# First attention's node table and turned edge lists moved ahead of the branch on the edge list's order

## Chip, cores and metric

The kernel runs on one core of a Trainium2 chip. The metric is device microseconds of one execution. The four runs of the kernel before have a median of 7833.06 us (7821.41 to 7836.81).

## What is computed

The input is a graph of 6250 nodes with 256 features each and a list of 206,250 edges (`src`, `dst`, sorted by `dst`). Four layers follow one another, and each adds its result to `x`. The change touches only the first one, a graph attention with 4 heads of 64 columns:

```
h = (layernorm(x) @ W).reshape(N, H, C)
a_src = einsum('nhc,hc->nh', h, att_src);  a_dst = einsum('nhc,hc->nh', h, att_dst)
e = leaky_relu(a_src[src] + a_dst[dst])
p = exp(e - segment_max(e, dst)[dst])
out = segment_sum(p / segment_sum(p, dst)[dst] * h[src], dst)
x = x + relu(out + bias)
```

After it come a mixture of 8 experts (top 2), a weighted sum over the same edges, and a second attention with a mixture of 4 experts.

## The kernel before, in words

The 6250 nodes are 49 tiles of 128 rows. `X` holds all of them in SBUF for the whole kernel; eight DMAs on the ACT queue load it (L2190, L2191). The kernel has two ways to compute the result: `fast` (from L1835), which relies on the edges being almost evenly spread over the sorted `dst`, and `general`, which doesn't. What decides is a look at the list.

**The look** is `check_stream` (L1032 to L1109). It copies `dst` into a padded DRAM list, reads it back shifted by one place and by other offsets (L1055, L1056, L1059, L1081, one after the other into two buffers), and compares on VectorE in tiles of 128x1664. On the way it writes the list as float (`dl_d`, L1069), as 16-bit integers (L1067), a mark of equal neighbours (L1060) and a mark of each node's last edge (`last_d`, L1072) to DRAM. Its last instruction writes `flag` (L1109). Each engine reads the flag into a register (L2197) and takes the branch.

**Behind the branch** `fast` first makes what the attention's stream needs. *The turned lists* (L1852 to L1868): `src` is loaded, negative or too large numbers are mended on VectorE, and `turn_rows` (L1111) transposes 13 blocks of 128x128 on TensorE, with ScalarE copying from PSUM; the same for `dl_d` (less the first node of each window, L1157 to L1176) and for `last_d`. The results `si`, `dl`, `il` stay in SBUF. *The table* (L1870 to L1896): `W` and the two attention vectors are loaded on the ACT queue, eight columns that give `a_src` and `a_dst` are made from them, and then the nodes go through in 7 chunks of 7 tiles: layernorm on VectorE (L247 to L257), two transposes per tile on TensorE and a copy on ScalarE (`transposed`, L259), two matmuls (L1890, four records a tile in the profile), a copy to `tb` on ScalarE (L1891), a copy of four columns to `NI` on VectorE (L1892), one store of each chunk to the DRAM tensor `tab` on the SP queue (L1893) and two small VectorE operations on `NI` (L1895, L1896).

**The stream** is `gat_stream` (L1191). It first splits `NI` into three bf16 parts (L1215 to L1219), writes them to DRAM (`s_nb`, L1221), and then runs in an order written out by hand: GpSimd gathers rows of `tab` by `si` (L1260, 1612 gathers), and the other engines work on pieces of 8 x 128 edges.

Outside that hand-written order, an automatic scheduler sets the order of each engine's instructions when the program is built: an instruction earlier in the program goes first, a later one fills in where the earlier is expected to wait. The order is then fixed, each engine runs its own in order, and nothing of a branch's body mixes with what stands outside it. DMAs issued on SP stand in SP's order, those issued on ACT in ScalarE's, between its copies. Buffers of pools that are open at different times share space, and the later one waits until the earlier is no longer in use.

Of the kernel before, what the change touches and what calls it, by code (L numbers as in the profile page):

```python
# [20 lines left out]
F32 = mybir.dt.float32  # L21
BF = mybir.dt.bfloat16
I32 = mybir.dt.int32
I16 = mybir.dt.int16
AF = mybir.ActivationFunctionType
OP = mybir.AluOpType
AX = mybir.AxisListType
PSUM = bass.MemoryType.PSUM
# [4 lines left out]
P = 128  # L33
LN_EPS = 1e-5
BIG = float(2**100)
CH = 7
# [11 lines left out]
def chunks(n, size):  # L48
    return [(i, min(size, n - i)) for i in range(0, n, size)]


def rows(ap):

    return bass.AP(tensor=ap.tensor, offset=ap.offset, ap=[[0, P], [1, ap.size()]])
# [17 lines left out]
def tile_kernel(ctx, tc, src_ins, out):  # L72
    nc = tc.nc
    x_in = src_ins["x"]
# [172 lines left out]
    def layernorm(pool, dst, src, n):  # L247

        mv = pool.tile([P, n, 2], F32, name="mv")
        for t in range(n):  # L250
            bs = pool.tile([P, 6], F32, name="bs")
            nc.vector.bn_stats(bs, src[:, t, :])
            nc.vector.bn_aggr(mv[:, t, :], bs)
        rs = rstd_of(pool, mv[:, :, 1], n)
        for t in range(n):
            nc.vector.tensor_scalar(dst[:, t, :], src[:, t, :], mv[:, t, 0:1], rs[:, t:t + 1],
                                    op0=OP.subtract, op1=OP.mult)  # L257

    def transposed(pp, dst, src, **bufs):  # L259

        pt = pp.tile([P, KD, P], F32, name="pt", **bufs)
        for k in range(KD):
            nc.tensor.transpose(pt[:, k], src[:, k * P:(k + 1) * P], ident)
        nc.scalar.copy(dst, pt)
# [405 lines left out]
    def x_rows(ap):  # L670

        for t0, n in chunks(FULL, CH):
            yield ap[t0 * P:(t0 + n) * P].rearrange("(t p) d -> p t d", p=P), X[:, t0:t0 + n, :]
        if REST:
            yield ap[FULL * P:], X[:REST, FULL, :]
# [435 lines left out]
    def turn_rows(dst, src, C):  # L1111

        with tc.tile_pool(name="turn_ps", bufs=2, space=PSUM) as pp:
            for c0, n in chunks(C, 4):
                pt = pp.tile([P, 4, P], F32, name="pt")
                for c in range(n):
                    nc.tensor.transpose(pt[:, c], src[:, c0 + c, :], ident)
                nc.scalar.copy(dst[:, c0 * P:(c0 + n) * P], pt[:, :n].rearrange("p c e -> p (c e)"))

    def load_rows(p, ap, E, C, dtype, name):  # L1120

        t = p.tile([P, C, P], dtype, name=name)
        nc.vector.memset(t[:, C - 1:, :], 0)
        a = C - 1
        nc.sync.dma_start(t[:, :a, :], ap[:a * P * P].rearrange("(c p e) -> p c e", p=P, e=P))
        left = E - a * P * P
        r = left // P
        if r:
            nc.sync.dma_start(t[:r, a, :], ap[a * P * P:a * P * P + r * P].rearrange("(p e) -> p e", p=r))
        if left > r * P:  # L1130
            nc.sync.dma_start(t[r:r + 1, a, :left - r * P], ap[a * P * P + r * P:E][None, :])
        return t
# [23 lines left out]

    def from_first_window(s, dl, p):  # L1157

        base = p.tile([P, s.C * P], F32, name="base")
        if s.group is None:  # L1160
            b0, start = s.windows(0, Q)[0][0], 0
            for q in range(-(-s.T // Q) + 1):
                b = s.windows(q * Q, min(Q, s.T - q * Q))[0][0] if q * Q < s.T else None
                if b != b0:
                    nc.gpsimd.memset(base[:, start:s.C * P if b is None else q * Q], float(P * b0))
                    b0, start = b, q * Q
        else:
            nc.gpsimd.memset(base[:, s.T:], 0.0)
            for i, n, first, step in s.runs:
                full = min(n, s.T // s.group - i)  # L1170
                if full > 0:
                    nc.gpsimd.iota(base[:, i * s.group:(i + full) * s.group], pattern=[[step, full], [0, s.group]],
                                   base=first, channel_multiplier=0, allow_small_or_imprecise_dtypes=True)
                if full < n:
                    nc.gpsimd.memset(base[:, (i + full) * s.group:s.T], float(s.wins[-1][0]))
        nc.vector.tensor_sub(dl, dl, base)  # L1176
# [655 lines left out]

    moves = {}

    def fast(flag_s0, last_d, dl_d):  # L1835
        s0 = flag_s0
        C = s0.C
        keep = ExitStack()
# [1 line left out]
        wide = moves["wide"] = kp.tile([P, 3 * P], F32, name="wide")  # L1840
        nc.vector.memset(wide, 0.0)
        nc.vector.tensor_copy(wide[:, P:2 * P], ident)
        tab = dram.tile([NP, D + H0], F32, name="tab")
        chosen_by = ExitStack()
        f0 = chosen_by.enter_context(tc.tile_pool(name="f0f", bufs=1))
        head = Head(f0)
        with tc.tile_pool(name="gat0f", bufs=1) as g0:
# [1 line left out]
            dl = g0.tile([P, C * P], F32, name="dl")  # L1849
            il = g0.tile([P, C * P], BF, name="il")  # L1850
            NI = g0.tile([P, NT, 2 * H0], F32, name="NI")
            with tc.tile_pool(name="rows", bufs=1) as p:  # L1852
                sr = load_rows(p, I["src"], s0.edges, C, I32, "sr")
                sf = p.tile([P, C, P], F32, name="sf")
                t = p.tile([P, C, P], F32, name="tt")
                nc.vector.tensor_copy(sf, sr)
                nc.vector.tensor_scalar(t, sf, 0.0, float(N), op0=OP.is_lt, op1=OP.mult)
                nc.vector.tensor_add(sf, sf, t)
                nc.vector.tensor_scalar(sf, sf, 0.0, float(N - 1), op0=OP.max, op1=OP.min)
                turn_rows(si, sf, C)  # L1860
                dr = p.tile([P, C, P], F32, name="dr")
                nc.sync.dma_start(dr, dl_d)
                turn_rows(dl, dr, C)
                from_first_window(s0, dl, p)
                lr = p.tile([P, C, P], F32, name="lr")
                nc.sync.dma_start(lr, last_d)
                turn_rows(il, lr, C)

            with tc.tile_pool(name="l0", bufs=2) as lp, tc.tile_pool(name="l0_ps", bufs=2, space=PSUM) as pp:
                wx = lp.tile([P, KD, D + 2 * H0], F32, name="wx", bufs=1)  # L1870
                nc.scalar.dma_start(wx[:, :, :D], I["L0_gnn_W"].rearrange("(k p) f -> p k f", p=P))
                att = lp.tile([P, 2, D], F32, name="att", bufs=1)
                nc.scalar.dma_start(att[:, 0], rows(I["L0_gnn_att_src"]))
                nc.scalar.dma_start(att[:, 1], rows(I["L0_gnn_att_dst"]))
                for k in range(KD):
                    for s in range(2):
                        pr = lp.tile([P, D], F32, name="pr")
                        nc.vector.tensor_mul(pr, wx[:, k, :D], att[:, s])
                        nc.vector.tensor_reduce(wx[:, k, D + s * H0:D + (s + 1) * H0],
                                                pr.rearrange("p (h c) -> p h c", h=H0), AX.X, OP.add)  # L1880
                for t0, n in chunks(NT, CH):
                    xl = lp.tile([P, CH, D], F32, name="xl")
                    layernorm(lp, xl, X[:, t0:t0 + n, :], n)
                    tb = lp.tile([P, CH, D + H0], F32, name="tb")
                    for j in range(n):
                        xT = lp.tile([P, KD, P], F32, name="xT")
                        transposed(pp, xT, xl[:, j, :])
                        ph = pp.tile([P, D + 2 * H0], F32, name="ph")
                        for k in range(KD):
                            nc.tensor.matmul(ph, xT[:, k], wx[:, k], start=(k == 0), stop=(k == KD - 1))  # L1890
                        nc.scalar.copy(tb[:, j, :], ph[:, :D + H0])  # L1891
                        nc.vector.tensor_copy(NI[:, t0 + j, :H0], ph[:, D + H0:])  # L1892
                    nc.sync.dma_start(tab[t0 * P:(t0 + n) * P].rearrange("(t p) d -> p t d", p=P), tb[:, :n])  # L1893
                    own = NI[:, t0:t0 + n, H0:]
                    nc.vector.tensor_add(own, tb[:, :n, D:], NI[:, t0:t0 + n, :H0])  # L1895
                    nc.vector.scalar_tensor_tensor(own, own, 0.2, own, op0=OP.mult, op1=OP.max)  # L1896
            bias = g0.tile([P, D], F32, name="bias")
            nc.sync.dma_start(bias, rows(I["L0_gnn_bias"]))

# [287 lines left out]

    if REST:
        nc.vector.memset(X[:, FULL, :], 0.0)
    for a, b in x_rows(x_in):  # L2190
        nc.scalar.dma_start(b, a)  # L2191
    s0 = Stream("s0", I["src"].shape[0], SLACK0, N, GROUP0, True)
    last_d = dram.tile([P, s0.C, P], F32, name="last_d")
    dl_d = dram.tile([P, s0.C, P], F32, name="dl_d")
    flag = main.tile([P, 1], I32, name="flag")
    check_stream(s0, I["dst"], flag, last_d, dl_d)
    v = nc.values_load(flag[0:1, 0:1], min_val=0, max_val=1, skip_runtime_bounds_check_because="a comparison: 0 or 1")  # L2197
    with tc.If(v == 1) as cmp:
        fast(s0, last_d, dl_d)
    with cmp.Else():  # L2200
        general()

# [22 lines left out]
```

## Time and profile before

| what | us |
|---|---|
| median of four runs | 7833.06 |
| the profiled execution, by its own time | 7850.32 |
| its span in the trace | 7848.5 |
| flag written | 66.35 to 66.51 |
| first instruction behind the branch (SP) | 67.44 |
| last turned list copied | 92.08 |
| first and last tile of the table (first transpose, last `NI` operation) | 98.80 to 170.10 |
| store of `s_nb` issued | 176.76 |
| first gather | 188.55 |

The times inside the execution count from the span's start. The profile lists busy time by engine, and for a group of instructions the time that its engine stood idle just before them and what ended this wait. PE is TensorE (PEld its weight loads), DVE is VectorE, ACT is ScalarE, POOL is GpSimd, SP issues DMAs; a `q` after the name means the engine's own queue of instructions, where DMA issues are. `PEclk` is the granted clock of TensorE as a share of full speed.

### The profile page before, as it was taken

What the parts mean: (1) busy time and instruction counts of PE and PEld (TensorE: products, weight loads), DVE (VectorE), ACT (ScalarE), POOL (GpSimd) and SP (SyncE); (2) the same over time, 40 slices, a digit from 0 to 9 for tenths busy, and PEclk for the clock granted to TensorE, in tenths of its full rate; (3) what the DMA queues carried; (4) which work ended last, traced back from release to release, by engine and by line L of the source; (5) the groups of instructions that cost most, each with busy time, mean ns of one, the idle gap of its engine ahead of it and who ended that gap; (6) DMA issues with size and microseconds to landing.
All of it is one profiled execution on the core that took longest, in us unless ns stands there. A gap on an engine that the chain in (4) does not pass through costs nothing.

```text
span 7848.5 us, 62325 instructions
## 1 busy us (share of the span) xinstructions
PE 3837.8 (49%) x17463; PEld 2905.0 (37%) x17463; DVE 4465.4 (57%) x10655; ACT 1160.3 (15%) x2758; POOL 4103.3 (52%) x4320
## 2 busy tenths in 40 slices
PE   3355555555555699994235555555555641111111
PEld 2244434343433488873123333343433421111110
DVE  4355555555555753434576666666766615665666
ACT  2011111111111123221001222221211210000000
POOL 0666666666666232320666666666666355555552
PEclk9677777776777799997567777777777865555555
DMA  4444444444444165575333333333333212222221
GB/s 126 117 120 121 119 116 113 113 119 115 121 116 118 55 204 187 185 227 179 98 93 100 96 100 100 101 101 96 99 99 97 72 41 46 50 47 46 46 49 41
DMA packets 496233, 821.82 MB, mean 105 GB/s; under 512 B 143345, under 2 KB 315588, under 8 KB 495843
## 3 DMA queue, kind: packets, MB, share of 16 engines
q0 software_dynamic: 190880, 462.26, 22.6%
q1 hardware_dynamic: 292326, 343.79, 14.3%
q10 hardware_dynamic: 12668, 11.68, 0.5%
q8 instruction: 141, 2.31, 0.1%
q14 instruction: 218, 1.78, 0.1%
HBM read 743.27 MB, written 77.29 MB: 105 GB/s over the span
## 4 chain that ended last, share of the span: by engine, by line
DVE 20%; PE 18%; another core or an unknown queue 13%; issue 9%; ACT 2%; DMA 2%; POOL 1%; ACTq 0%; DVEq 0%; SPq 0%; POOLq 0%
DVE run L2028 8%; PE ph L630 5%; PE py L643 5%; PE pf L1714 3%; PE pf L1725 3%; DVE X L1813 2%; DVE oh L1152 2%; PE acc L2142 1%; DVE run L2026 1%; DVE s L1345 1%; DVE g L1347 1%; DVE ot L1270 1%; DVE oh L2032 1%; ACT h L1719 0%
## 5 line engine op out<-in xcount | busy, mean ns | idle before, releaser
L234 POOL DMA_INDIRECT g<-tab_ef,si x1616 | 1540.7, 953 | 1028.0 <-issue 563.2
L1260 POOL DMA_INDIRECT g<-tab,si x1612 | 1542.5, 957 | 907.4 <-issue 544.6
L2028 DVE SCALAR_TENSOR_TENSOR run<-g,wab,run 128x256 f32<-128x256 f32 x2626 | 1264.8, 488 | 540.1 <-DVE run L2028 185.8
L1260 POOL DMA_INDIRECT g<-tab_1f,si1s x787 | 761.6, 968 | 716.6 <-issue 626.5
L1363 PE MATMUL acc<-g,oh 128*128 128x264 f32 x3224 | 989.4, 467 | 190.8 <-DVE g L1340 103.8
L1363 PEld LDWEIGHTS acc<-g,oh 128*128 128x128 f32 x3224 | 751.0, 239 | 382.5 <-DVE g L1340 117.4
L1290 DVE TENSOR_REDUCE nd<-pd 128x64 f32<-128x192 f32 (+1 forms) x301 | 106.0, 352 | 1212.6 <-remote 959.5
L1714 PE MATMUL pf<-xt,w 128*128 128x512 f32 (+1 forms) x832 | 486.7, 724 | 464.8 <-ACT h L1719 193.2
L2142 PE MATMUL acc<-run,oh 128*128 128x256 f32 x808 | 295.2, 500 | 681.0 <-DVE oh L2032 315.7
L1725 PE MATMUL pf<-w,h 128*128 128x256 f32 x1568 | 413.1, 414 | 223.1 <-ACT y L1730 93.6
L2142 PEld LDWEIGHTS acc<-run,oh 128*128 128x128 f32 x808 | 191.7, 250 | 784.1 <-issue 409.7
L1340 DVE TENSOR_TENSOR g<-g,mix 128x2048 f32<-128x2048 f32 x202 | 457.6, 2265 | 0.0
L1714 PEld LDWEIGHTS pf<-xt,w 128*128 128x128 f32 x832 | 183.4, 241 | 661.3 <-issue 310.8
L1363 PE MATMUL acc<-s,oh 128*128 128x72 bf16 x1267 | 97.0, 251 | 672.0 <-DVE s L1345 510.8
L1725 PEld LDWEIGHTS pf<-w,h 128*128 128x128 f32 x1568 | 316.1, 207 | 292.9 <-issue 104.2
L1306 PE MATMUL zt<-ident,Z 128*128 128x128 f32 x228 | 76.9, 396 | 681.3 <-ACT Z L1298 393.0
L630 PE MATMUL ph<-xe,w 128*128 128x256 f32 x1792 | 406.9, 384 | 5.1 <-DVE xe L618 5.1
L643 PE MATMUL py<-w,h 128*128 128x256 f32 x1792 | 397.3, 379 | 0.0
L630 PEld LDWEIGHTS ph<-xe,w 128*128 128x128 f32 x1792 | 342.3, 193 | 52.1 <-DVE xe L618 5.9
L643 PEld LDWEIGHTS py<-w,h 128*128 128x128 f32 x1792 | 335.7, 190 | 43.1
L1363 PEld LDWEIGHTS <-oh 128*128 128x128 bf16 x1267 | 90.4, 133 | 675.6 <-issue 581.7
L606 POOL DMA_INDIRECT xg<-tab_x,gi x112 | 126.8, 1132 | 389.1 <-PE pt L615 314.7
(506 smaller groups left out, 5931.8 us busy)
## 6 DMA issues: line engine op xcount, KB each, us to landing
w<-in_L_ffn_W SPq DMA_DIRECT2D x112, 1024.0 KB
db<-s_d SPq DMA_DIRECT2D x299, 256.0 KB
g<-tab_ef,si POOLq DMA_INDIRECT x1616
g<-tab,si POOLq DMA_INDIRECT x1612
y_d<-y SPq DMA_DIRECT2D x196, 128.0 KB
yb<-y_d SPq DMA_DIRECT2D x49, 512.0 KB
g<-tab_1f,si1s POOLq DMA_INDIRECT x787
yy<-tab_y SPq DMA_DIRECT2D x7, 1792.0 KB
```

Source lines behind the costliest of these rows:

```text
L234: nc.gpsimd.indirect_dma_start(out=dst, out_offset=None, in_=table, in_offset=bass.IndirectOffsetOnAxis(ap=si[:, t:t + 1], axis=0))
L630: nc.tensor.matmul(ph, w1[:, k, f * P:(f + 1) * P], xe[:, k, :], start=(k == 0), stop=(k == KD - 1))
L643: nc.tensor.matmul(py, hs[f][:, i * P:(i + 1) * P], w2[:, f, :], start=(f == 0), stop=(f == FC - 1))
L1152: nc.vector.tensor_tensor(o[:, :m], ips[:, None, k * P:(k + 1) * P].to_broadcast([P, m, P]), dl[:, a:a + m, None].to_broadcast([P, m, P]), ...
L1260: nc.gpsimd.indirect_dma_start(out=g[:, j, :DH + H], out_offset=None, in_=tab, in_offset=bass.IndirectOffsetOnAxis(ap=si[:, t0 + j:t0 + j ...
L1340: nc.vector.tensor_mul(gh, gh, ps[0][:, o:o + n, :, None].to_broadcast([P, n, H, CD]))
L1363: nc.tensor.matmul(acc[b].rearrange("p s w -> p (s w)"), oh[:, t - a], m_, start=(t == lo), stop=(t == hi))
L1714: nc.tensor.matmul(ph[:, :n], w1[:, e, k, f * P:(f + 1) * P], xts[g][:, k, :n], start=(k == 0), stop=(k == KD - 1))
L1725: nc.tensor.matmul(py[:, :D], hs[g, e, f][:, j * P:(j + 1) * P], w2[:, e, f, :], start=(f == 0), stop=(f == FC - 1))
L1813: nc.vector.scalar_tensor_tensor(X[:, b, :], v[:, e, :], gates[:, j, e:e + 1], X[:, b, :], op0=OP.mult, op1=OP.add)
L2028: nc.vector.scalar_tensor_tensor(at[:, i] if j < Q - 1 else r[i], g[:, j, :], w, at[:, i], op0=OP.mult, op1=OP.add)
L2142: nc.tensor.matmul(acc[i], oh[:, k], r[k], start=(q % 2 == 0 and k == 0), stop=(last and k == 1))
```

## The change

The layernorm, the table and the turned lists are taken out of `fast` and put into one block with `check_stream`, ahead of the flag's reading. They therefore run whatever the flag says. The pools of that block are open together, so that the look, the lists and the table have buffers of their own.

What was kept in SBUF now goes through DRAM: `si`, `dl`, `il` are stored (`si_d0`, `dl_d0`, `il_d0`), `NI` is stored chunk by chunk (`ni_d`), and `fast` loads the four of them. On the ACT queue `W` and the two attention vectors are loaded ahead of `X`. The copy from PSUM takes all 264 columns in place of 260, and the four columns of `NI` are then copied once a chunk in place of once a tile. Some buffers are used again: `src`'s own tile takes the turned `si`, and the tiles `tt` and `sf` take `dl_d` and `last_d`.

```diff
     def fast(...):
...
-            with tc.tile_pool(name="rows", bufs=1) as p:
-                sr = load_rows(p, I["src"], s0.edges, C, I32, "sr")
...
-            with tc.tile_pool(name="l0", bufs=2) as lp, tc.tile_pool(name="l0_ps", bufs=2, space=PSUM) as pp:
...
-                        nc.scalar.copy(tb[:, j, :], ph[:, :D + H0])
-                        nc.vector.tensor_copy(NI[:, t0 + j, :H0], ph[:, D + H0:])
...
+            for t, d in ((si, si_d0), (dl, dl_d0), (il, il_d0)):
+                nc.sync.dma_start(t, d)
+            nc.sync.dma_start(NI.rearrange("p t d -> p (t d)"), ni_d)
...
-    for a, b in x_rows(x_in):
-        nc.scalar.dma_start(b, a)
...
-    check_stream(s0, I["dst"], flag, last_d, dl_d)
+    tab = dram.tile([NP, D + H0], F32, name="tab")
+    ni_d = dram.tile([P, NT * 2 * H0], F32, name="ni_d")
+    with tc.tile_pool(name="l0", bufs=2) as lp, tc.tile_pool(name="l0_ps", bufs=2, space=PSUM) as pp:
+        wx = lp.tile([P, KD, D + 2 * H0], F32, name="wx", bufs=1)
+        nc.scalar.dma_start(wx[:, :, :D], I["L0_gnn_W"].rearrange("(k p) f -> p k f", p=P))
+        att = lp.tile([P, 2, D], F32, name="att", bufs=1)
+        nc.scalar.dma_start(att[:, 0], rows(I["L0_gnn_att_src"]))
+        nc.scalar.dma_start(att[:, 1], rows(I["L0_gnn_att_dst"]))
+        for a, b in x_rows(x_in):
+            nc.scalar.dma_start(b, a)
+        check_stream(s0, I["dst"], flag, last_d, dl_d)
...
+        si = load_rows(p, I["src"], s0.edges, C, I32, "sr")
...
+        turn_rows(si, sf, C)
+        nc.sync.dma_start(si_d0, si)
+        dl = p.tile([P, C * P], F32, name="dl", bufs=1)
+        nc.sync.dma_start(t, dl_d)
+        turn_rows(dl, t, C)
+        from_first_window(s0, dl, p)
+        nc.sync.dma_start(dl_d0, dl)
+        il = p.tile([P, C * P], BF, name="il", bufs=1)
+        nc.sync.dma_start(sf, last_d)
+        turn_rows(il, sf, C)
+        nc.sync.dma_start(il_d0, il)
...
+        for t0, n in chunks(NT, CH):
+            xl = lp.tile([P, CH, D], F32, name="xl")
+            layernorm(lp, xl, X[:, t0:t0 + n, :], n)
+            tb = lp.tile([P, CH, D + 2 * H0], F32, name="tb")
+            for j in range(n):
...
+                nc.scalar.copy(tb[:, j, :], ph)
+            nc.sync.dma_start(tab[t0 * P:(t0 + n) * P].rearrange("(t p) d -> p t d", p=P), tb[:, :n, :D + H0])
+            ni = lp.tile([P, CH, 2 * H0], F32, name="ni")
+            own = ni[:, :n, H0:]
+            nc.vector.tensor_copy(ni[:, :n, :H0], tb[:, :n, D + H0:])
...
+            nc.sync.dma_start(ni_d[:, 2 * H0 * t0:2 * H0 * (t0 + n)], ni[:, :n].rearrange("p t d -> p (t d)"))
     v = nc.values_load(flag[0:1, 0:1], ...)
     with tc.If(v == 1) as cmp:
-        fast(s0, last_d, dl_d)
+        fast(s0, si_d0, dl_d0, il_d0, tab, ni_d)
```

## The prediction

> **What bounds the kernel now.** Most of the span is gathers and what hangs on them; the change lies in the first 188.55 us, before the first gather. So I read that stretch, first by stages: the look, the lists, the table, the preparation of the stream, the stream.
>
> ```profile
> core 0: us, PE busy (x) PEld busy (x) DVE busy (x) ACT busy (x) POOL busy (x), PEclk, DMA share, GB/s
> 0.00:67.40 67.40, 0.58 (x2) 0.50 (x2) 30.34 (x29) 0.00 (x0) 2.18 (x7) 1.00 0.65 196
> 67.40:91.50 24.10, 9.62 (x39) 7.43 (x39) 8.12 (x8) 6.39 (x12) 2.33 (x6) 1.00 0.33 111
> 91.50:170.10 78.60, 62.73 (x294) 48.24 (x294) 49.58 (x226) 35.84 (x109) 0.00 (x0) 0.96 0.23 79
> 170.10:188.55 18.45, 0.00 (x0) 0.00 (x0) 3.02 (x6) 0.00 (x0) 0.59 (x6) 0.51 0.71 67
> 188.55:2400.00 2211.45, 1113.65 (x5066) 856.31 (x5066) 1140.10 (x2220) 244.69 (x683) 1399.19 (x1463) 0.72 0.44 118
> ```
>
> The stages stand one behind the other. In the first, TensorE and ScalarE do nothing and VectorE is busy for 30.3 of 67.4 us; in the third, TensorE is nearly full (62.7 of 78.6). What VectorE waits for ahead of the flag is seen in its waits:
>
> ```profile
> DVE d L1066 <- DMA lend<-s_dst: 16.9, 1, 16.9
> DVE t L1071 <- DMA lend<-s_dst: 8.4, 1, 8.4
> DVE kf L1058 <- DMA lend<-s_dst: 5.6, 1, 5.6
> DVE t L1082 <- DMA lend<-s_dst: 3.2, 1, 3.2
> ```
>
> These 34.1 us are the look's own round trips through DRAM, and they are room. What the table costs an engine stands in the groups of instructions of the first 190 us (count, busy us, mean ns, idle before):
>
> ```profile
> L1890 PE MATMUL ph<-wx,xT 128*128 128x264 f32 x196 | 51.3, 405 | 7.5 <-ACT xT L264 7.5
> L252 DVE BATCH_NORM_STATS2 bs<-X 128x6 f32<-128x256 f32 x49 | 18.5, 415 | 1.3 <-PE pt L1117 1.3
> L256 DVE TENSOR_SCALAR xl<-X,mv,rs 128x256 f32<-128x256 f32 x49 | 17.4, 410 | 1.1 <-PE pt L263 1.1
> L263 PE MATMUL pt<-ident,xl 128*128 128x128 f32 x98 | 15.4, 279 | 7.3 <-issue 7.3
> L1892 DVE COPY NI<-ph 128x4 f32<-128x4 f32 x49 | 7.8, 160 | 26.7 <-ACT tb L1891 26.1
> L253 DVE BATCH_NORM_AGGREGATE mv<-bs 128x2 f32<-128x6 f32 x49 | 6.7, 167 | 0.0
> ```
>
> TensorE's 51.3 + 15.4 us are the table's floor, and VectorE's wait of 26.1 us for ScalarE's copies says that it is not the bound there. The end of the stretch, in order of time:
>
> ```profile
> 169.91 0.19 DVE L1896 SCALAR_TENSOR_TENSOR NI<-NI 128x28 f32<-128x28 f32 x1
> ...
> 173.74 0.56 DVE L1215 CAST NB<-NI 128x392 bf16<-128x392 f32 x1 [3.43 <-DMA tab<-tb]
> ...
> 176.76 0.36 SPq L1221 DMA_DIRECT2D s_nb<-NB  x1
> ...
> 188.55 1.11 POOL L1260 DMA_INDIRECT g<-tab,si  x1 [14.11 <-DMA s_nb<-NB]
> ```
>
> From the table's end (170.10) it is 3.64 us to the split of `NI` and 18.45 to the first gather.
>
> **Rule of the sum.** From the first gather on the same instructions follow in the same hand-written order, so the change in time is the shift of the first gather. Call T the end of the table and lists after the change, and R what the split then waits. The shift is (T - 170.10) + (R - 3.64).
>
> **What is moved, by engine.** VectorE: the mending of `src` is 1.03 + 1.03 + 1.89 + 1.03, the subtraction 1.89, together 6.9 us; the eight columns 4 x (0.419 + 0.414) = 3.3; layernorm 18.5 + 6.7 + 17.4 + 1.3 for the reciprocals = 43.9, or 6.3 a chunk; the `NI` operations 3 a chunk at 0.18 (by L1895) in place of 49 copies. With the look's 30.3 that makes 88 us. The 6.5 us saved on copies are worth nothing, since VectorE was waiting there. ScalarE: 36 us of copies, and four columns more in each tile's copy (376 ns for 260) add 0.3 us in all; it waited 34.6 us for matmuls, so nothing again. TensorE: a pair of tiles takes 2.79 us (the second matmul groups start at 142.81 and 145.60), so 49 tiles 68.4 us; the turns 9.7 us (39 records in the first 24.1 us stage, 9.62). GpSimd: its five fills (2.3 us) stand in 64.7 us of idle time. SP: seven stores of the table, five loads and six stores of lists, seven of `ni_d` now stand in the same queue as the look's reads. ACT's queue: three loads ahead of `X`.
>
> **When TensorE can start.** The eight issues of `X` hold ScalarE's queue from 0.75 to 23.5 us, and each tile needs a ScalarE copy, so the table starts at about 25 us at best.
>
> **How much is done before the flag.** The look is earlier in the program, so on VectorE the layernorm has only its gaps: 34.1 us, of which the first 10 pass before `X`'s first chunk is there (an estimate: the DMAs moved 230 to 285 GB/s in that time, some 2.6 MB of mixed traffic). In the other 24 the columns (3.3) and the mending (5.0) come first, which leaves 16 us: 2.5 chunks at 6.3. The two buffers of the normalized rows allow two chunks ahead of TensorE as well. From 50 to 66 us VectorE is full, and TensorE, which needs 9.8 us a chunk, runs dry.
>
> **The flag and after.** `src`, `W` and the vectors (805 + 256 + 256 KB) come into the window in which DMA was full (285 to 385 GB/s); 1.3 MB at 330 is 4 us, so the flag comes at 70.4. Then TensorE has 9.7 us of turns (they need the look's last outputs and VectorE is at the next layernorm meanwhile) and the rest of the table: T = 70.4 + 9.7 + (49 - 7k) x 1.394 + 1.1 for the last copies, with k chunks done before. k = 2: 130.2; k = 3: 120.5; middle 125.3.
>
> Here the Trainium skill speaks against the change. The look's first reads took 9.6 us (issued at 10.04 and 10.49, landed by 20.08) beside `X`, and the last one 5.3 us (41.73 to 47.07) with nothing beside it. The page "DMA: Bandwidth & Descriptors", section "Issuing engines are not separate DMA queues", says that the DMAs of all queues run on the same 16 engines and interleave. By that rule two more reads of the look would take the longer time beside the table's stores, 2 x 4.3 us more, and the forecast below would be 9 us later.
>
> **What is added behind the branch.** SP takes the branch 1.1 us after its last issue (66.35 to 67.44 before), issues Head's two loads (0.85), then `si`, `dl`, `il` and `NI`, 2.28 MB. The nearest row are the three list loads before: 2.4 MB from 68.37 until the turn's start at 79.39, 11.0 us. Adding 0.4 for the issue of the last `ni_d` store, R = 13.4, which is 9.8 more than now. The lower end is a small load, 3.06 us (`att`, 92.71 to 95.77): R = 5.4, 1.8 more. Behind `NI`'s load SP holds `bias`, `s_nb` and the first loads of the stream; before, those stood behind `s_nb`'s landing too, so nobody else waits. I take 9.8, as the sizes are alike. The stores of the lists (2 MB) lie beside the table and cost nothing unless they lie between the look's reads.
>
> **Sum.** (125.3 - 170.1) + 9.8 = -35 us. The profiled execution's 7850.3 becomes 7815; it stands 17.3 above the median, which becomes 7833 - 35 = **7798 us**.
>
> **Rivals.**
> 1. *Everything overlaps*: VectorE serves both, and TensorE alone sets the end: 25 + 68.4 + 9.7 = 103. Shift -67.0 + 9.8 = -57, time 7776. For it: 34 us of gaps. Against: VectorE's 88 us leave little slack and the look's dense stretch comes in one piece.
> 2. *It doesn't do what it says*: the fixed order puts the layernorm behind the look (k = 0), or SP's order puts the look's reads behind stores that wait for matmuls. T = 149.5, shift -11, time 7822: no measurable difference. For it: before, the layernorm stood behind other things in every queue, and the order is set at build time from expected durations, while the reads took up to 9.6 us.
> 3. *Slower, by TensorE's clock.* Where TensorE had been idle the table began slowly: from 98 to 102 us the granted clock was 0.50, four transposes took 1.19 instead of 0.60 us and the first eight matmuls 3.05 instead of 2.05, so a pair 4.24 instead of 2.79. If the starved TensorE stayed there for the table, rival 2's 68.4 us become 104: T = 185, shift +25, time 7858. It decides from T above 176 on (shift over +15.7). For it: from 190 to 280 us, at some 5% busy, the clock was 0.50, and 0.73 to 0.76 at 50 to 60%. Against: in the table itself, 90% busy, it was 1.00, and after the flag TensorE is fed without a break.
>
> The page "TensorE: Matmul & The Clock Gate", section "What's actually happening", has it that the gate opens after about 3.4 us of sustained work and closes after an idle window of that length. In the trace the clock was back at 0.99 from 102 us on, 3.2 us after the first transpose, and had fallen to 0.54 in the stretch from 95 us on, after TensorE's last turn at 91.5. By the rule each chunk that TensorE starts after a pause costs one slow pair, 1.5 us, so two pauses 3 us, and rival 3 cannot hold.
>
> **Numbers.** Forecast (k from 1 to 4) 0.58, rival 1 0.17, rival 2 0.17, rival 3 0.08. A measurement of this kernel tells 0.2% (15.7 us) from no change. k = 1 gives T = 140 and -20.6, still faster; so faster 0.58 + 0.17 = 0.75, same 0.17, slower 0.08. The range runs from rival 1 with the small R (-65, 7768) to rival 2 with 6 us for a second slow read (7828) and leaves rival 3 out.
>
> **What would show it.** Right: transposes of layernormed rows (L263 before) from about 25 us on, a pause of TensorE until the flag, VectorE's four waits of the look filled in part, the last tile near 125, the first gather near 151. Wrong: a first transpose behind the flag (rival 2), a clock of 0.5 over tens of us (rival 3), the last tile near 103 (rival 1), or a stream that doesn't keep its 2211 us.

## The result, and the profile after

The median after is 7817.62 us (44 runs, 7788.62 to 7868.94), before 7832.67 us (68 runs, 7790.19 to 7864.72). The ratio is 0.9983, 95% interval 0.9974 to 0.9991: 13 us less, between 7 and 20, against 35 forecast. That is less than the 0.2% that the prediction called telling. The two profiled executions differ by 52 us (span 7796.3 after 7848.5). Most of this isn't the change's: the runs of one kernel spread over 75 us, and single executions say nothing at this size. The first gather tells more, because the stretch ahead of it repeats within 0.4 us (170.72 here, 170.38 in a second profile of the same kernel).

The stretch by stages, cut at the flag, the table's end, the split of `NI` and the first gather (columns as before):

```profile
core 0: us, PE busy (x) PEld busy (x) DVE busy (x) ACT busy (x) POOL busy (x), PEclk, DMA share, GB/s
0.00:74.20 74.20, 11.89 (x45) 7.74 (x45) 45.47 (x85) 6.77 (x17) 4.43 (x13) 1.00 0.71 212
74.20:140.70 66.50, 58.32 (x291) 45.54 (x290) 33.02 (x135) 34.06 (x102) 0.00 (x0) 0.97 0.38 127
140.70:154.97 14.27, 0.00 (x0) 0.00 (x0) 0.83 (x4) 0.10 (x1) 0.59 (x5) 0.60 0.70 242
154.97:170.70 15.73, 0.00 (x0) 0.00 (x0) 2.82 (x5) 0.00 (x0) 0.00 (x0) 0.50 0.73 19
170.70:2620.00 2449.30, 1241.69 (x5660) 956.64 (x5660) 1281.95 (x2511) 277.15 (x771) 1542.44 (x1612) 0.72 0.44 117
```

Ahead of the flag TensorE was busy for 11.9 us only, and six of the table's seven chunks still stand behind it (28 of its 196 matmul records lie ahead). The stream's 2449.3 us compare with 2450.5 before (from 188.5 to 2639): it kept its length in these two executions. VectorE's waits ahead of the flag show why TensorE had so little:

```profile
DVE d L1066 <- DMA lend<-s_dst: 9.5, 1, 9.5
DVE t L1071 <- DMA lend<-s_dst: 9.3, 1, 9.3
DVE pr L2190 <- DMA att<-in_L_gnn_att_src: 5.9, 1, 5.9
DVE kf L1058 <- DMA lend<-s_dst: 2.1, 1, 2.1
DVE t L1082 <- DMA lend<-s_dst: 0.6, 1, 0.6
```

27.4 us of waiting stayed, where the kernel before had 34.1; 5.9 of the 27.4 are a new wait, for `att`, ahead of the look's first read. The second of these waits, with what follows on VectorE (and ScalarE's square root), in order of time:

```profile
31.71 1.89 DVE L1058 TENSOR_TENSOR kf<-lend,lend 128x1664 bf16<-128x1664 int32 x1 [2.12 <-DMA lend<-s_dst]
...
33.60 0.49 ACT L242 ACTIVATE sd<-mv,eps 128x7 f32<-128x7 f32 x2
...
42.89 1.89 DVE L1071 TENSOR_TENSOR t<-lend,lend 128x1664 f32<-128x1664 int32 x1 [9.29 <-DMA lend<-s_dst]
...
50.29 0.19 DVE L244 RECIPROCAL rs<-sd 128x7 f32<-128x7 f32 x1
...
57.36 0.41 DVE L256 TENSOR_SCALAR xl<-X,mv,rs 128x256 f32<-128x256 f32 x1
57.82 0.69 PE L263 MATMUL pt<-ident,xl 128*128 128x128 f32 x2 [57.82 <-DVE xl L256]
58.62 0.41 DVE L256 TENSOR_SCALAR xl<-X,mv,rs 128x256 f32<-128x256 f32 x1
```

At 34.1 the square roots of two chunks are there, and VectorE stands idle for 9.3 us; but in its fixed order the reciprocal and the normalizing (L244, L256) come behind the look's L1071, and then one tile at a time between the look's steps of 1.9 us. The end of the stretch:

```profile
140.54 0.19 DVE L2209 SCALAR_TENSOR_TENSOR ni<-ni 128x28 f32<-128x28 f32 x1
140.75 0.45 SPq L2210 DMA_DIRECT2D ni_d<-ni  x1
145.23 0.38 SPq L691 DMA_DIRECT2D wr<-in_L_ffn_Wr  x1
...
147.59 0.62 SPq L1853 DMA_DIRECT2D NI<-ni_d  x1
...
154.97 0.56 DVE L1215 CAST NB<-NI 128x392 bf16<-128x392 f32 x1 [8.76 <-DMA NI<-ni_d]
...
157.96 0.38 SPq L1221 DMA_DIRECT2D s_nb<-NB  x1
...
170.72 1.11 POOL L1260 DMA_INDIRECT g<-tab,si  x1 [24.84 <-DMA s_nb<-NB]
```

So the table's end T is 140.73 (forecast 125.3), the wait R from there to the split is 14.24 (13.4), and from the split to the gather it is 15.75 (14.81 before). The shift of the first gather is 170.72 - 188.55 = -17.8 us, which lies in the interval of the timed runs.

### The profile page after: what moved, and what is told of

Its sections match the earlier page's. It is cut to its first block, busy times and chain, and to the rows that moved or that the text cites. A ratio compares the mean times of both kernels' runs of the same rounds, so it can differ in the third digit from the quotient of the medians.

```text
span 7796.3 us, 62291 instructions
## 1 busy us (share of the span) xinstructions
PE 3846.9 (49%) x17463; PEld 2906.3 (37%) x17463; DVE 4458.3 (57%) x10613; ACT 1158.6 (15%) x2757; POOL 4100.2 (53%) x4320
## 3 DMA queue, kind: packets, MB, share of 16 engines
q0 software_dynamic: 190880, 462.26, 22.6%
## 4 chain that ended last, share of the span: by engine, by line
DVE 28%; PE 26%; another core or an unknown queue 21%; issue 15%; ACT 3%; DMA 3%; POOL 2%; ACTq 1%; DVEq 0%; POOLq 0%; SPq 0%
DVE run L1985 7%; PE acc L1363 5%; PE ph L630 5%; PE py L643 5%; PE pf L1714 4%; DVE oh L1152 3%; DVE g L1340 3%; PE pf L1725 2%; POOL g L1260 2%; DVE X L1813 2%; DVE ot L1270 1%; PE acc L2099 1%; DVE run L1983 1%; PE bacc L1389 1%
```

## The experiments

Theory after the result: the change is worth the shift of the first gather and nothing else; T is late because VectorE's fixed order puts the normalizing behind the look, so that one chunk of seven was done at the flag. Rivals: ScalarE, held by the issues of `X` until 32.3 us, delays the table; VectorE has too much work in all; the stream absorbs or adds something. Times are compared with runs of the kernel before on the same chip only: the first and third group ran where that kernel takes 6481 to 6483 us, the second where it takes 7767 us.

**NI loaded first** (first group, one run).

```diff
+            nc.sync.dma_start(NI.rearrange("p t d -> p (t d)"), ni_d)
             for t, d in ((si, si_d0), (dl, dl_d0), (il, il_d0)):
                 nc.sync.dma_start(t, d)
-            nc.sync.dma_start(NI.rearrange("p t d -> p (t d)"), ni_d)
```

> The changed kernel with one edit: behind the branch the load of NI is issued ahead of the loads of si, dl and il. Theory (the split of NI waits for the 2 MB of lists in front of it on SP's queue): the table still ends near 140.7 and the branch is taken near 145.2, but the split starts near 150 in place of 154.97, and the first gather near 166 in place of 170.72, since the lists land beside the split and the store of s_nb. Rival (the four loads share the same transfer engines, so NI lands no earlier, or si becomes what the first gather waits for): split at 154 to 155, or first gather still at 170 to 171.

The split, on VectorE in order of time:

```profile
149.59 0.56 DVE L1215 CAST NB<-NI 128x392 bf16<-128x392 f32 x1 [3.22 <-DMA NI<-ni_d]
```

It starts 5.4 us earlier, the wait ahead of it is 3.2 in place of 8.8, and the first gather comes at 166.0. Of the round trip, 5 us were the place in the queue. The time was 6457.0 against 6481.3 (one run).

**Table first** (first group, five runs). The columns and the loop over the chunks are moved ahead of `check_stream`; no instruction is added or taken out.

```diff
+        for k in range(KD):
...
+        for t0, n in chunks(NT, CH):
...
         check_stream(s0, I["dst"], flag, last_d, dl_d)
...
-        for k in range(KD):
...
-        for t0, n in chunks(NT, CH):
...
```

> The changed kernel with the same instructions in another order of the program: columns and table first, then the look, then the lists. Theory (the table is late because VectorE's fixed order puts the normalizing behind the look): first transpose near 42 in place of 57.8, TensorE fed from there on, end of the block near 117 to 122 in place of 140.7, first gather near 150, time 20 us (0.25%) below the changed kernel, ratio to the kernel before 0.995 to 0.997. Rival (VectorE is the bound once both are mixed, as it has 88 us of work): end of the block at 130 or later and first gather within 10 us of 170.72, ratio about 0.998.

Its stages, up to the first transpose, the table's end and the branch:

```profile
0.00:44.40 44.40, 0.00 (x0) 0.00 (x0) 20.33 (x59) 1.77 (x3) 4.43 (x13) 1.00 0.99 287
44.40:116.80 72.40, 66.14 (x317) 51.76 (x317) 54.94 (x159) 35.45 (x108) 0.00 (x0) 1.00 0.37 123
116.80:127.20 10.40, 2.71 (x18) 1.97 (x18) 1.91 (x2) 3.53 (x9) 0.00 (x0) 0.90 0.90 341
```

From the first transpose on TensorE is busy for 66 of 72 us while VectorE does 55 us of both kinds of work beside it. The table ends at 116.8 in place of 140.7 although the flag comes at 102.4 in place of 74.1, because nothing waits for the flag before the block's end. The branch is taken at 127.15 (the turned lists are last now), the first gather at 152.4. The ratio is 0.9944 (0.9931 to 0.9958): 36 us less, the shift of the first gather from 188.55 (which was measured on a slower chip; the kernel before has no trace on this one). The first gather comes 18 us earlier than in the changed kernel with the same work in another order, so VectorE's total isn't the bound. The look's waits were not filled here either: VectorE still waits 22.9 us ahead of the flag (6.0 for `att`, 13.8 and 3.1 for the look's reads). What moved is the look's dense stretch, which now gives way to the normalizing.

**X issued on GpSimd's queue** (first group, one run).

```diff
         for a, b in x_rows(x_in):
-            nc.scalar.dma_start(b, a)
+            nc.gpsimd.dma_start(b, a)
```

> The changed kernel with one edit: the eight loads of X are issued on GpSimd's queue instead of ScalarE's. Theory (VectorE's order): ScalarE is free early, but the normalizing still stands among the look's instructions, so at most one chunk more is done by the flag: end of the table 131 to 141. Rival (ScalarE, held by the issues of X until 32.3 us, is what delays the table): first transpose near 20 to 25 in place of 57.8 and end of the table at 120 or earlier.

The first transpose comes at 42.0, but the table ends at 139.6, and the first gather comes at 168.8:

```profile
41.57 2.33 DVE L256 TENSOR_SCALAR xl<-X,mv,rs 128x256 f32<-128x256 f32 x7
...
65.13 0.41 DVE L256 TENSOR_SCALAR xl<-X,mv,rs 128x256 f32<-128x256 f32 x1
67.25 0.41 DVE L256 TENSOR_SCALAR xl<-X,mv,rs 128x256 f32<-128x256 f32 x1
```

These are VectorE's normalizings: the first chunk 16 us earlier, the second still one tile at a time between the look's steps. The edit did more than free ScalarE: the look's first read landed at 32.3 in place of 26.9 and the flag came at 78.7 in place of 74.1, so this run alone doesn't settle the rival. Two others do: in the table-first kernel the issues of `X` stood on ScalarE's queue as in the change (until 25.2, there until 32.3) and the table ended at 116.8, and with two chunks first (below) they held it longer, until 34.3, while the first transpose came 12.5 us earlier than in the change. The queue can hold the first chunk up; it doesn't set the table's end.

**Only the table ahead** (first group, one run): the lists are made behind the branch as before.

```diff
-        si = load_rows(p, I["src"], s0.edges, C, I32, "sr")
...
+            with tc.tile_pool(name="rows", bufs=1) as p:
+                sr = load_rows(p, I["src"], s0.edges, C, I32, "sr")
...
```

> The changed kernel with one part undone: the turned lists are made behind the branch as in the kernel before; only the table is ahead. Theory (the lists' part earns nearly nothing, since their round trip through DRAM and the turns beside the table cost about what it saves, and behind the branch the lists lie beside the round trip of NI and s_nb): the table ends near 134 to 136, the first gather lies within 5 us of the changed kernel's 170.72. Rival (the lists' 24 us come back in full): first gather near 185 to 190.

The table ended at 126.1, earlier than expected, and the first gather came at 169.2. The split stood behind the turns there:

```profile
153.81 0.56 DVE L1215 CAST NB<-NI 128x392 bf16<-128x392 f32 x1 [1.27 <-PE pt L1117]
```

So the hoisted lists earn nothing in the changed kernel (170.7 with them, 169.2 without). With them the branch comes 15.0 us later (145.23 and 130.20), and from the branch to the split it takes 9.7 us in place of 23.6, 13.9 less. Of the 14.7 us that they add to T (140.7 less 126.1), the turns are 6.2 and the later flag is 2.8 (74.1 and 71.3); the other 5.7 go with one chunk less ahead of the flag, since without the lists two were done by then (56 matmul records in place of 28).

**Table and NI first** (second group, five rounds): both edits together.

> The changed kernel with the table ahead of the look in the program and the load of NI ahead of the lists. Theory (both gains are shifts of the first gather and add up): first gather near 147.7 (152.4 of the table-first kernel less the 4.7 of the NI-first kernel), that is 41 us before the 188.55 of the kernel before, and the time lower by the same 41 us within 5. Rival (the stream behind absorbs part of a shift, for instance because its own first transfers fall differently): less than 30 us lower.

First gather at 147.55, 41.0 us earlier than before. Ratio 0.9949 (0.9925 to 0.9973), 40 us less with 21 to 58 in the interval. The two gains add up; the time agrees, if widely.

**The split ahead of the branch too** (second group, five rounds): beyond the change, table first, and the three parts of `NI` made and stored chunk by chunk.

```diff
+            nc.vector.tensor_copy(nbt[:, :n, 0], ni[:, :n])
+            nc.vector.tensor_sub(r[:, :n], ni[:, :n], nbt[:, :n, 0])
...
+            nc.sync.dma_start(ni_d[t0 * P:(t0 + n) * P].rearrange("(t p) d -> p t d", p=P),
+                              nbt[:, :n].rearrange("p t s d -> p t (s d)"))
...
-            nc.sync.dma_start(NI.rearrange("p t d -> p (t d)"), ni_d)
```

> Beyond the change: table first, and NI is split into its three bf16 parts and stored as s_nb chunk by chunk ahead of the branch, so that neither NI's round trip nor the 12 us store of s_nb stands behind the branch. Theory (behind the branch it was this chain that held the first gather): the branch is taken near 128, the first gather follows once si is loaded, near 135, and the time is 53 us below the kernel before. Rival (VectorE's 35 more instructions and the small pieces of the store hold the table up, or the gather then waits for dl and il as well): first gather at 145 or later.

The branch and the first gather, on GpSimd:

```profile
130.52 0.59 POOL L1182 IOTA s_nid<- 128x1 f32 x5 [125.44 <-DMA s_il<-il]
136.81 1.10 POOL L1259 DMA_INDIRECT g<-tab,si  x1 [5.71 <-DMA si<-s_si]
```

The first gather waits for `si` last and comes at 136.8, 51.7 us earlier than before. Ratio 0.9926 (0.9901 to 0.9952), 57 us less: the fastest version here. Now the lists, not the table, end the block.

**A store of X added** (second group, one run), meant to stand last in the block.

```diff
+        nc.sync.dma_start(x_d, X.rearrange("p t d -> p (t d)"))
     v = nc.values_load(flag[0:1, 0:1], ...)
```

> The changed kernel with one store added ahead of the branch, of all of X (6.4 MB) into a DRAM tensor that nobody reads. Theory (the first instruction behind the branch on every engine waits for all transfers issued before it, needed or not; this is why the branch took 4.1 us after SP's last issue in place of 1.1): the branch is taken near 162 to 165 in place of 145.2, and the first gather comes near 188. Rival (an engine waits only for what it reads): branch near 145, first gather below 180, as the lists are only loaded more slowly beside the store.

It doesn't answer its question: the scheduler issued the store at 42.88, where `X` was ready. The look's flag came at 96.75 in place of 74.1, yet the table ended at 130.9 and the first gather came at 160.0, 10.7 us earlier than without the store. The order on VectorE was another one as well, so this only shows once more that a late look needn't mean a late table.

**A copy of the table added** (third group, one run), which cannot be issued before the table has landed.

```diff
+        nc.sync.dma_start(tab_2[NP // 2:], tab[NP // 2:])
     v = nc.values_load(flag[0:1, 0:1], ...)
```

> The changed kernel with one transfer added at the end of the block: the second half of the table (3.3 MB) is copied from DRAM to DRAM into a tensor that nobody reads; it can only be issued once the last store of the table has landed, near 145. Theory (the first instruction behind the branch on every engine waits for all transfers issued before it, needed or not): the branch is taken 10 us or more later than 145.2, near 158, on all engines at once, and the first gather near 184. Rival (an engine waits only for what it reads): the branch near 146 to 147, after SP's issue of the copy, and the first gather within 8 us of 170.7.

VectorE and SP behind the block:

```profile
145.37 0.54 SPq L2212 DMA_DIRECT2D tab<-tab  x1
...
145.70 0.38 DVE L1841 MEMSET wide<- 128x384 f32 x1 [4.65 <-DMA ni_d<-ni]
...
147.05 0.38 SPq L691 DMA_DIRECT2D wr<-in_L_ffn_Wr  x1
```

VectorE goes on at 145.7 and SP 1.1 us after its issue: nobody waits for the copy, so the theory that the branch waits for every transfer falls. It does wait for the stores of `tb` and `ni`, whose buffers give their space to the pools behind the branch; that this is the reason is likely and wasn't tried. The first gather came at 181.2, later than the rival had it: the load of `NI` was issued 2.2 us later and took 8.4 us longer beside the copy, so that the split started at 165.56.

**The changed kernel once more** (second group, five rounds).

> The changed kernel itself once more, beside its variants. Theory (the change is worth the shift of the first gather, 17.8 us, and all behind it is the same): 15 to 21 us below the kernel before in the same runs. Rival (the 52 us by which the two profiled executions differ is the change's, in the weighted sum's gathers): 40 us or more below.

Ratio 0.998 (0.9961 to 0.9998), 16 us less with 2 to 30 in the interval; the rival's 40 lie outside. The theory is borne out only loosely, as the two medians differ by no more than 2 us (7764.6 and 7766.6).

**Two chunks first** (third group, one run): the columns and the first two chunks ahead of the look, five behind.

```diff
+        for t0, n in chunks(NT, CH)[:2]:
+            table(t0, n)
         check_stream(s0, I["dst"], flag, last_d, dl_d)
...
+        for t0, n in chunks(NT, CH)[2:]:
+            table(t0, n)
```

> The changed kernel with the columns and the first two of the table's seven chunks ahead of the look in the program, the other five where they were. Theory (the end of the table is the flag, the turns, and 1.394 us for each tile that isn't done by then; the changed kernel has one chunk done): two chunks done by the flag, which itself comes up to 5 us later than 74.1, so the end of the table lies at 131 to 136 in place of 140.7 and the first gather at 161 to 166. Rival (VectorE's work is conserved, so what is done earlier for the table delays the flag by as much): end of the table at 139 or later.

The flag came at 79.4 and the table's end at 138.0, between the two expectations; the first gather at 167.6. Two chunks were done at the flag, but VectorE had put both behind the look's long wait again (first transpose at 45.3):

```profile
42.80 1.89 DVE L1071 TENSOR_TENSOR t<-lend,lend 128x1664 f32<-128x1664 int32 x1 [7.17 <-DMA lend<-s_dst]
...
44.84 4.61 DVE L256 TENSOR_SCALAR xl<-X,mv,rs 128x256 f32<-128x256 f32 x14
```

So the 14 normalizings delayed the flag by 5.3 us instead of filling that wait. The gain of a chunk is 2.7 us of T and not 9.8; the later flag takes 5.3 of the difference, and the other 1.8 stays open. Of the orders tried, only the one in which the look yields to the whole table (table first) keeps TensorE fed.

## Why the prediction was wrong

- *The rule of the sum* held. On the faster chips the first stream took 2033 to 2036 us from its first gather to its last in all six variants, wherever between 152.4 and 181.2 the first one came. Over the kernels with several runs the time went with the first gather: shifts of -17.8, -36.1, -41.0 and -51.7 us stand beside 13 (7 to 20) and 16 (2 to 30), 36 (27 to 45), 40 (21 to 58) and 57 us (37 to 77) less. The single runs of NI first, X on GpSimd, only the table, the table's copy and two chunks first agree less closely: shifts of -22.6, -19.8, -19.4, -7.4 and -20.9 beside 24, 12, 18, 0 and 25 us less. The added store's single run (47 us less at a shift of -28.5) says little, as the kernel before spread over 71 us on that chip.
- *"Which leaves 16 us: 2.5 chunks at 6.3"* is the step that failed. It took the look's waits for room. They stayed waits (27.4 us), because VectorE runs its order and what was ready behind a waiting instruction didn't overtake it (from 34.1 to 42.9). They stayed in the table-first order too (22.9 us), so the gain there came from the order and not from filling them. With one chunk done in place of 2.5 the same formula gives 1.5 x 9.76 = 14.6 us more; T was 15.4 us over.
- *The flag* came at 74.1 in place of 70.4, 3.7 us more. The look's first read took 15.4 us (issued at 11.50, landed by 26.90) in place of 9.6 to 10, now beside `src` as well as `X`. This agrees with the page "DMA: Bandwidth & Descriptors" (section "Issuing engines are not separate DMA queues"), by which the DMAs of all queues run on the same 16 engines and interleave. But the sum by the page put 4.3 us on each of the two later reads, beside stores of the table. The first such store was issued at 72.3, behind them, and they took only 0.9 us more each (9.3 in place of 8.4 and 6.2 in place of 5.3 from issue to use). That sum's flag would have been 79; the measurement lies between the two.
- *The turns* cost TensorE 6.2 us (4.3 + 1.9) in place of 9.7, which takes back 3.5: a turn took 273 ns in place of 421. The granted clock in the traces doesn't explain this (1.00 around the turns before, 0.82 to 1.00 here), so the cause stays open. That this and the late flag nearly cancel is luck.
- *"The table starts at about 25 us at best"*: it started at 57.8. ScalarE was held longer, by 30.07 us of issues in place of 22.78, and then VectorE's order came on top.
- *R* was 14.24 against 13.4, but made up otherwise: the branch 4.5 us after the table's end in place of 1.5, the loads 8.8 in place of 11.0. That the split to the gather stayed equal was off by 0.9.
- *The lists* were costed as a part of the block and never by themselves; in the changed kernel they earn nothing.
- *The rivals*: neither the full overlap nor the slow clock came (0.97 granted from the flag to the table's end). Rival 2 named the mechanism, an order set at build time from expected durations, but as all or nothing; what came is one chunk, nearer to it (T 149.5) than to the middle.
- *Slips without weight*: the formula for T gives 130.0, 120.2 and a middle of 125.1, where 130.2, 120.5 and 125.3 were written; and the lists have three stores, not six.

Summed: -35 + 15.4 + 0.8 + 0.9 = -17.9, the measured shift of -17.8 but for rounding.

## What to carry to other kernels

Idle time of an engine with a fixed order is room only for instructions that stand ahead of the waiting one: before counting it, ask which instruction is next in the order. Where two pieces of work share an engine and one feeds the engine that sets the end, put that one first in the program, even if the other's result comes later. And what is hoisted over the branch here pays a round trip through DRAM and a place in a queue behind it; hoist the longest chain, and load what is needed first, first.

## What the runs showed of the hardware

- Issuing a load isn't free for the engine whose queue it is on: the eight issues of `X` (six of 896 KB, one of 768, one of 106) held ScalarE's queue for 22.8 us before and 30.1 us after the change. On GpSimd's queue they took 7.3 us.
- The kernel before took 6481 to 6483 us on two chips and 7767 to 7833 us on others. The stretch ahead of the gathers isn't where they differ: in kernels with the same instructions up to the branch it was taken at 145.4 on a faster chip (NI first) and at 145.2 and 145.7 on the slower ones (the changed kernel). The difference lies in the gathers' stages: from the first to the last of the 1612 gathers of the first stream it took 2033 to 2036 us on the faster chips and 2412 to 2461 us on the slower ones, with the same 0.95 us for each and more idle time between them. In two variants of this kernel, the NI-first one on a faster chip and the changed one in the second group:

```profile
L1260 POOL DMA_INDIRECT g<-tab,si x1612 | 1543.5, 958 | 511.1 <-issue 424.0 <-DVE Z L1296 28.3 <-DMA s_nb<-NB 19.9
```

```profile
L1260 POOL DMA_INDIRECT g<-tab,si x1612 | 1534.1, 952 | 929.1 <-issue 564.2 <-ACT lo L703 143.0 <-PE pd L1281 75.1
```

The idle time ahead of the gathers is 511 us in the one and 929 us in the other. What holds the other engines up there stays open.
